# A conv, state-space and attention kernel: two empty steps in the routing, keys fetched one group earlier, and the last two blocks divided in SBUF

## The chip, the cores and the metric

The kernel runs on one core of a Trainium2 chip, in fp32. The metric is the device time of one execution in microseconds. An execution of the kernel before took 5163.62 us (median of three).

## What is computed

The input is an image batch `x` of shape (4, 128, 64, 64). Two residual layers follow each other. Cut to what matters:

```python
# layer 0
x = x + conv_ref(group_norm(x))        # LN, depthwise 3x3 conv, LN, gelu, 1x1 conv, LN,
                                       # a selective scan (16 states) over 4 channel chunks, LN, projection
# layer 1, on tokens (4, 4096, 128)
t = tokens(x)
t = t + attention(ln(t))               # 4 heads of 32, softmax over 4096 keys
t = t + moe(ln(t))                     # 8 experts, the best 2 of a softmax, weights made to sum to 1
x = image(t)
```

Attention divides the weighted sum of values by the sum of the exponentials. The kernel gets both from one matrix product: the values carry columns of ones, so the rows of the accumulator `av` hold, for each of two query blocks, 32 rows of sums and 32 rows that all hold the denominator. The expert part computes, for every token, the sum over the eight experts of (weight x token) times the expert's matrix; weights of unchosen experts are zero.

## The kernel before, in words

**Units.** Each of the 4 batches has 4096 tokens, handled as 8 blocks of 512 (`BLK`). The scan of a block takes 32 slots; a *slot* is one turn of the main loop, and 1024 slots (`END`) hold all scan work. Attention lags behind the scan, because its keys, queries and values come from finished blocks; it goes on for 132 slots after the scan has ended (the *drain*), and a *tail* of expert work follows when attention is done too.

**Order.** Every instruction is issued through one helper (`queued`; all records of the profile carry its line, 406), which chains each engine's instructions in the order of emission. So each engine works strictly in the order in which the slot loop emits. In a slot, that order is: sends that are due; the fetch of scan rows (`rows`, from `bcd`, on SP); the decays (`da`, ACT); on even slots the driven input (`h<-rows,du`, DVE); a second half of a stage on lane X; the scores (`sc`) of the next attention group on PE and their exponentials (`pT`) on ACT; the scan (2.35 us of DVE) on even slots or the product `hc<-rows,h` (1.22 us of DVE) on odd ones; a first half on lane Y; `y<-ident,hc`, by which PE sums an earlier `hc` over its states; a second half on lane Y; the value products (`av`) of the group of the slot before; a first half on lane X.

**Lanes.** All other work is cut into stages at each `yield` of a generator. Two lanes, X and Y, run one task each, two stages for each slot (`advance`): the first, third, ... stage of a task in its first half, the next in its second half. An empty stage lets time pass. Each lane has one PSUM bank for its work (`ps_X`, `ps_Y`). Tasks on lane X are `closed(b, i)`, which ends a block of layer 0 and makes its keys, queries (both as `hi` and `lo` parts) and values (`vst`), and `finished(b, qb, lane)`, called an "out" task: it takes one 512-token block of attention output, divides it (`aT`, `inv`), projects it, adds the residual (`acc`), routes it and applies the experts. An out task may start only in slots 2 to 17 of a block's 32, and only while enough parts of the attention are ready. In the drain and after it both lanes take out tasks. A chain of some 18 small DVE operations in `finished` finds the best two experts and leaves weights in `bothX` or `bothY`; PE transposes those, ACT copies them to `prT`, a DMA stores the weights in DRAM, and DMAs bring them back spread over all partitions (`share`).

**Attention.** The work of a batch is a list of *parts*: a pair of query blocks (`qs`), a head, and one or two blocks of keys (`ks`, `v`). A part of one block has two *groups*, a part of two blocks four; one group is done in each slot (4 passes of PE for `sc`, 8 for `av`). `ready` says whether the blocks that a part needs are closed. The next part's operands are fetched by SP at a set distance from the end of a part; where they were not ready then, the loads are tried again at each group, and at a part's start if need be. Three buffers hold `ks` and `v`, two hold `qs`. Partial sums go to DRAM (`avd`) and come back (`prev`).

**Division.** After the last head of a query pair, the sums of all four heads lie in DRAM (`total`). `inverted` loads the denominators in a compact form (`den`), inverts them, stores them (`inverse`); `finished` loads them spread (`inv`) and multiplies.

The lines that change are shown in these functions:

Of the kernel before, what the change touches and what calls it, by code (L numbers as in the profile page):

```python
# [9 lines left out]
F32 = mybir.dt.float32  # L10
# [7 lines left out]
P = 128  # L18
C = 128
EPS = 1e-5  # L20
BLK = 512
NT = BLK // P
# [3 lines left out]
DH = 32  # L26
NH = 4
NE = 8
# [8 lines left out]
def conv_mamba_attn_moe_kernel(ctx: ExitStack, tc: tile.TileContext, t: dict):  # L37
    nc = tc.nc
    x, out = t["x"], t["out"]
    B, _, L = x.shape  # L40
    NB = L // BLK
# [11 lines left out]
    def load(name, shape=None, src=None, eng=nc.sync, pool=const):  # L53
        src = t[name] if src is None else src
        w = pool.tile(list(shape or src.shape), F32, name=f"w_{name}")
        eng.dma_start(out=w, in_=src)
        return w
# [25 lines left out]
    wv, wp, rw, ew, eb8 = (load(k, eng=late) for k in ("wv", "wp", "rw", "ew", "eb8"))  # L83
# [13 lines left out]
    for j in range(4):  # L97
        r = slice(DI * (j % 2), DI * (j % 2) + DI)
# [301 lines left out]
    class Queue:  # L400
# [7 lines left out]
    tensor, vector, scalar, gpsimd, sync = (  # L408
        Queue(e) for e in (nc.tensor, nc.vector, nc.scalar, nc.gpsimd, nc.sync)
    )  # L410

    def mm(out, lhsT, rhs, start=True, stop=True):
        tensor.matmul(out, lhsT=lhsT, rhs=rhs, start=start, stop=stop)
# [24 lines left out]
    def pool(name, bufs=1, space=None):  # L438
        return main.enter_context(
            tc.tile_pool(name=name, bufs=bufs, **({} if space is None else {"space": space}))  # L440
        )

    att, mix, side = pool("att"), pool("mix"), pool("side")
# [4 lines left out]
    def work(lane, shape=None):  # L448
        return ps_work.tile(shape or [P, BLK], F32, tag=f"work{lane}", name=f"ps_{lane}")

    def tmp(lane, name, shape=None):
        return side.tile(
            shape or [P, BLK], F32, tag=f"tmp{lane}", name=name, bufs=6 if lane == "X" else 4
        )
# [417 lines left out]
    STEP = 2  # L872
# [57 lines left out]
    def attention(b):  # L930

        seen, parts = {}, []
        for q, lo, hi in RUNS:
            known = seen.get(q, 0)
            seen[q] = known + hi - lo
            cuts = [lo, *range(lo + 2 - lo % 2, hi, 2), hi]
            for h in range(NH):  # L940
                for k0, k1 in zip(cuts, cuts[1:]):
                    parts.append((
                        q, h, k0 // 2, k0 % 2, k1 - k0, k0 == lo, k1 == hi, known > 0,
                        seen[q] == NB,
                    ))
        assert all(n == NB for n in seen.values())

        def load(part, qs=None):
            q, h, k, u, n = part[:5]
            if qs is None:  # L950
                qs = queries(b, q, h)
            return qs, keys(b, h, k, u, n), values(b, h, k, u, n)

        prev = None
        ahead = None
        for at, part in enumerate(parts):
            q, h, k, _, n, first, last, more, final = part
            position[0] = b, parts, at
            if ahead is None:
                while not ready(b, part):  # L960
                    yield None
                ahead = load(part)
                for _ in range(2):
                    yield None
            qs, ks, v = ahead
            ahead = None
            for g in range(0, NT * n, STEP):
                if g == 0 and last:
                    prev = None
                    if more:  # L970
                        prev = att.tile([P, BLK], F32, name="prev", bufs=2)
                        sync.dma_start(out=prev, in_=partial.pop((b, q, h)))
                if g >= NT * n - 3 * STEP and ahead is None and at + 1 < len(parts):
                    nxt = parts[at + 1]
                    if ready(b, nxt):
                        ahead = load(nxt, qs if nxt[:2] == (q, h) and not nxt[5] else None)
                scs = []
                for j in range(g, g + STEP):
                    sc = ps_sc.tile([P, 2, BLK], F32, name="sc")
                    for u in range(2):  # L980
                        mm(
                            sc[:, u, :], ks[:, j * P : (j + 1) * P],
                            qs[:, u * BLK : (u + 1) * BLK],
                        )
                    scs.append((v[:, j // NT, j % NT, :], sc))
                yield (
                    b, q, h, scs, first and g == 0, last and g + STEP == NT * n, prev, final,
                )

    sums, partial, total, inverse, later = [None], {}, {}, {}, deque()  # L990
# [9 lines left out]
    def weighted(group):  # L1000
        b, q, h, pTs, first, last, prev, final = group
        if first:
            sums[0] = ps_av.tile([P, BLK], F32, name="av")
        av = sums[0]
        for k, (v, pT) in enumerate(pTs):
            for u in range(2):
                mm(
                    av[64 * u : 64 * u + 2 * DH, :], v, pT[:, u, :],
                    first and k == 0, last and k == STEP - 1,
                )  # L1010
        if last:
            avs = att.tile([P, BLK], F32, name="avs", bufs=2)
            if prev is None:
                scalar.copy(avs, av)
            else:
                vector.tensor_add(avs, av, prev)


            if not final:
                partial[b, q, h] = dram.tile([P, BLK], F32, name=f"avd{q}{h}")  # L1020
                send(partial[b, q, h], avs, 3)
                return
            if h == 0:
                total[b, q] = dram.tile([2, 2, NH, DH, BLK], F32, name=f"total{q}")
            d = total[b, q]
            send(d[:, :, h].rearrange("u k r q -> (u k) r q"), avs, 3)
            if h == NH - 1:
                work_left = inverted(b, q)
                later.extend((slot + n, work_left) for n in (4, 6, 8))

    def inverted(b, q):

# [15 lines left out]
            ))  # L1048
        yield

    def finished(b, qb, lane):

        q, u = divmod(qb, 2)
        td = kqv[b][3]
        s = slice(qb * BLK, (qb + 1) * BLK)
        acc = side.tile([P, NT, C], F32, name="acc", bufs=2)
        aT, inv = tmp(lane, "aT"), tmp(lane, "inv")
        sync.dma_start(out=aT, in_=total[b, q][u, 0].rearrange("h d q -> (h d) q"))
        sync.dma_start(
            out=inv, in_=inverse[b, q][u][:, None, :].to_broadcast([NH, DH, BLK])  # L1060
        )
        sync.dma_start(out=acc.rearrange("p j c -> p (j c)"), in_=td[:, s])
        yield
        yield
        yield
        vector.tensor_mul(aT, aT, inv)
        yield
        ps = work(lane, [P, NT, C])
        for j in range(NT):
            mm(ps[:, j, :], aT[:, j * P : (j + 1) * P], wp)  # L1070
# [4 lines left out]
        ps = transposed(lane, acc)  # L1075
        yield
        xf = tmp(lane, "xf")
        scalar.copy(xf, ps)
        yield
        ps = work(lane, [P, NT, NE])  # L1080
# [41 lines left out]
        vector.tensor_mul(both[:, :, 0:NE], pr, top1.to_broadcast(wide))  # L1122
        vector.tensor_mul(both[:, :, NE:], both[:, :, 0:NE], rs[:, :, None].to_broadcast(wide))
        yield

        ps = work(lane)
        for j in range(NT):
# [2 lines left out]
        prT = tmp(lane, "prT")[0 : 2 * NE, :]  # L1130
# [16 lines left out]


        ps = work(lane)
        mm(ps, eb8, prT[0:NE, :])  # L1150
        yield
        res = tmp(lane, "res")
        vector.tensor_add(res, ps, xf)
        yield
        ahead = deque(share(e) for e in (0, 2))
        yield
        yield
        for e in range(0, NE, 2):
            if e + 4 < NE:
                ahead.append(share(e + 4))  # L1160
            yield
            w = ahead.popleft()
            if e:
                vector.tensor_add(res, res, ps)
            vector.tensor_mul(w, w, xf[:, None, :].to_broadcast([P, 2, BLK]))
            yield
            ps = work(lane)
            for u in range(2):
                mm(ps, ew[:, e + u, :], w[:, u, :], u == 0, u == 1)
        yield  # L1170
        vector.tensor_add(res, res, ps)
        send(out[b][:, s], res, 2)
        yield

# [94 lines left out]
    lanes, done, running = {"X": deque(), "Y": deque()}, set(), {}  # L1269
# [50 lines left out]
    X, Y = lanes["X"], lanes["Y"]  # L1320
# [9 lines left out]
    for k in range(-2, len(blocks)):  # L1330
        if 0 <= k:
            b, i = blocks[k]
            Y.append((("in", b, i, 1), inputs(b, i, 1), [("scan", *blocks[k - 1], 1)] if k else []))
        if k + 2 < len(blocks):
            b, i = blocks[k + 2]
            if k + 2 == 0 or i > 0:
                upper(k + 2)
        if 0 <= k + 1 < len(blocks):
            b, i = blocks[k + 1]
# [19 lines left out]
    END = 2 * len(units)  # L1359

    rows, due, closing, y_of = {}, deque(), deque(), {}
    h_of, slot = {}, 0
# [18 lines left out]
    while (  # L1381
        slot < END or due or closing or summing or waiting or left or later or lanes["X"] or running
    ):
        at, odd = divmod(slot, 2)
# [10 lines left out]
        if unit and not odd:  # L1395
            h = h_of.pop(at)
# [44 lines left out]
    with tc.If(nc.values_load(general[0:1, 0:1]) > 0):  # L1441
# [4 lines left out]
        with tc.For_i(0, B, 1) as b:  # L1446
# [3 lines left out]
                out=t_tok.rearrange("p k c -> p (k c)"),  # L1450
                in_=tsave[bass.ds(b, 1)].rearrange("o p q -> (o p) q"),
            )
            with tc.tile_pool(name="ps_again", bufs=4, space=PSUM) as psum:
                for i in range(NB):
                    ps = anew(t_tok[:, NT * i : NT * (i + 1), :], psum)
# [92 lines left out]
```

## Time and profile before

| | |
|---|---|
| three runs | 5181.4, 5163.62, 5158.14 us; median 5163.62 |
| the profiled execution's own time | 5160.79 us |
| its span | 5158.6 us |
| granted TensorE clock, mean | 0.96 |
| busy: PE, DVE, ACT, POOL | 91%, 74%, 73%, 8% |
| first 645 us | filling: first blocks, attention starts |
| 645 to 4516 us | scan and attention together (the *middle*) |
| 4516 to 5086 us | attention alone (the drain) |
| 5086 to 5158.6 us | the tail |

The page gives the busy share of each engine over the whole span; the windows give it for each stretch. The waits list for one engine what its idle time ended with, in total, in times, and the longest. The chain of waits follows back from the last instruction to what released each step. A timeline row has start, length, engine, operation, and in brackets the idle time before it with what ended it. Consecutive rows of one engine overlap a little[...].

### The profile page before, as it was taken

The page shows a single profiled execution, that of the slowest core. Times are in us where ns is not written, and L with a number is a line of the kernel's source. Part 1 is how long each engine was busy: PE and PEld are TensorE (multiplying, and loading weights), DVE is VectorE, ACT ScalarE, POOL GpSimd, SP SyncE. Part 2 cuts the span into 40 slices and gives each one's busy share as a digit, 9 for nine tenths or more (in the row PEclk, how much of TensorE's full clock was granted, in tenths as well). Part 3 has the DMA queues.
Part 4 walks back from the last instruction along what each step waited for, and adds up shares of the span by engine and source line. Part 5 has one row for each costly group of instructions (what it writes and reads, how often), then busy time and mean ns, then how long its engine had stood idle before and what let it go on. Part 6 is the DMA issues. An engine that isn't in the chain of part 4 may idle for free.

```text
span 5158.6 us, 62573 instructions
## 1 busy us (share of the span) xinstructions
PE 4703.0 (91%) x20684; PEld 2317.3 (45%) x20684; DVE 3835.7 (74%) x5780; ACT 3743.0 (73%) x5700; POOL 433.5 (8%) x483
## 2 busy tenths in 40 slices
PE   4567898999999999999999999999999999999997
PEld 2333444444444444444444444444444444443443
DVE  6988767877778878877788787877888887752422
ACT  4556777887787777787878787787788787765453
POOL 1111111110000110010000100010000001000000
PEclk7778999999999999999999999999999999999997
DMA  4556567677666667676766767667866667764532
GB/s 127 182 189 214 206 212 253 234 235 244 232 226 226 232 230 255 230 241 234 265 236 207 235 218 273 239 227 245 286 219 221 221 234 258 239 212 163 177 130 68
DMA packets 451692, 1131.70 MB, mean 219 GB/s; under 512 B 51857, under 2 KB 135330, under 8 KB 451362
## 3 DMA queue, kind: packets, MB, share of 16 engines
q1 hardware_dynamic: 447296, 1125.96, 64.5%
q8 instruction: 166, 2.72, 0.2%
q10 hardware_dynamic: 4066, 1.67, 0.1%
q14 instruction: 164, 1.34, 0.1%
HBM read 967.22 MB, written 143.39 MB: 215 GB/s over the span
## 4 chain that ended last, share of the span: by engine, by line
PE 58%; DVE 17%; ACT 11%; DMA 7%; issue 4%; POOL 2%; SPq 1%; DVEq 0%; ACTq 0%; POOLq 0%
PE av L406 25%; PE sc L406 14%; PE ps_X L406 9%; PE ps_Y L406 6%; PE y L406 6%; DVE h L406 6%; ACT pT L406 4%; ACT L406 3%; DMA ks<-kd 2%; DVE hc L406 2%; DMA rows<-bcd 1%; ACT xt L406 1%; POOL rsX L406 1%; DMA inv<-inverse 1%; DVE stX L406 1%
## 5 line engine op out<-in xcount | busy, mean ns | idle before, releaser
L406 ACT ACTIVATE pT<-sc 128x1024 f32<-128x1024 f32 x2048 | 1984.9, 1023 | 923.4 <-PE sc L406 922.3
L406 PE MATMUL av<-pT,v 128*64 128x512 f32 x8192 | 2003.1, 610 | 6.4 <-DVE avs L406 6.3
L406 PE MATMUL sc<-qs,ks 128*128 128x512 f32 x4096 | 1298.7, 436 | 91.3 <-DMA ks<-kd 47.8
L406 DVE TENSOR_TENSOR_SCAN h<-da,state,h 128x1025 f32<-128x1025 f32 x512 | 1204.2, 2352 | 91.8 <-ACT h L406 58.2
L406 PEld LDWEIGHTS sc<-qs,ks 128*128 128x128 f32 x4096 | 701.1, 190 | 820.2 <-ACT pT L406 272.7
L406 PEld LDWEIGHTS av<-pT,v 128*64 128x64 f32 x8192 | 500.5, 137 | 838.6 <-issue 813.5
L406 ACT ACTIVATE da<-delta,amat 128x512 f32<-128x512 f32 x1024 | 744.4, 731 | 1.9
L406 PE MATMUL y<-ident,hc 128*128 128x128 f32 x4096 | 622.3, 283 | 58.4 <-DVE hc L406 58.4
L406 DVE TENSOR_TENSOR hc<-rows,h 128x1024 f32<-128x1024 f32 x512 | 624.4, 1220 | 15.7 <-PE y L406 5.4
L406 DVE TENSOR_TENSOR h<-rows,du 128x1024 f32<-128x1024 f32 x512 | 623.4, 1218 | 13.0 <-DMA rows<-bcd 13.0
L406 PEld LDWEIGHTS y<-ident,hc 128*128 128x128 f32 x4096 | 520.8, 147 | 219.0 <-issue 76.0
L406 POOL TENSOR_TENSOR rsX<-rsX,mhalf 128x4 f32<-128x4 f32 x92 | 203.7, 2214 | 2668.0 <-DVE rsX L406 2588.7
L406 ACT ACT_TABLE_LOAD x319 | 409.3, 1283 | 19.5 <-DVE zs L406 14.3
L406 POOL TENSOR_TENSOR rsY<-rsY,mhalf 128x4 f32<-128x4 f32 x100 | 132.1, 1321 | 1812.0 <-DVE shiftY L406 1358.4
L406 DVE TENSOR_TENSOR avs<-av,prev 128x512 f32<-128x512 f32 x96 | 66.1, 689 | 224.4 <-PE av L406 201.4
L406 PE MATMUL ps_X<-share,w_ew 128*128 128x512 f32 x432 | 216.0, 623 | 4.1 <-DVE share L406 3.9
L406 ACT ACTIVATE xt<-ps_Y,shiftY,rsY 128x128 f32<-128x128 f32 x380 | 143.9, 471 | 78.4 <-POOL shiftY L406 70.5
L406 DVE TENSOR_TENSOR share<-share,xf 128x1024 f32<-128x1024 f32 x128 | 155.9, 1218 | 23.5 <-DMA share<-sharesX 13.9
L406 DVE SCALAR_TENSOR_TENSOR cm<-y,w_fc1w,cm 128x512 f32<-128x512 f32 x195 | 145.0, 744 | 8.0 <-ACT y L406 4.5
L406 DVE TENSOR_TENSOR res<-res,ps_X 128x512 f32<-128x512 f32 x108 | 73.7, 683 | 99.9 <-PE ps_X L406 99.7
L406 PE MATMUL ps_Y<-pairs,inxc 128*128 128x512 f32 x256 | 131.2, 638 | 15.8 <-DMA pairs<-xn 10.2
L406 ACT COPY state<-h 128x2 f32<-128x2 f32 x448 | 88.9, 198 | 75.5 <-DVE h L406 75.5
(248 smaller groups left out, 3446.4 us busy)
## 6 DMA issues: line engine op xcount, KB each, us to landing
rows<-bcd SPq DMA_DIRECT2D x1024, 512.0 KB
ks<-kd SPq DMA_DIRECT2D x192, 512.0 KB
qs<-qd SPq DMA_DIRECT2D x161, 512.0 KB
share<-sharesX SPq DMA_DIRECT2D x108, 512.0 KB
v<-vd SPq DMA_DIRECT2D x192, 256.0 KB
ks<-kd SPq DMA_DIRECT2D x128, 256.0 KB
avd<-avs SPq DMA_DIRECT2D x96, 256.0 KB
prev<-avd SPq DMA_DIRECT2D x96, 256.0 KB
```

The lines of the kernel that those rows point to most:

```text
L406: return lambda *args, **kw: queued(op(*args, **kw))
```

## The change

1. **Routing.** Two empty stages stand between the chain on DVE and PE's transposition of its result. With them, an out task is one slot longer.
2. **Keys.** The next part's operands may be fetched from four groups before the end of a part, where it was three.
3. **The last two blocks.** The last query pair of the last batch no longer goes through DRAM. `divided` takes each head's sums as they leave the accumulator, inverts the whole tile (denominators stand 32 times, so every row has its own) and multiplies each block's 32 rows into a tile of the out task. `finished` takes that tile, and does not wait for stages that load and multiply.
4. **Experts after the scan.** From slot `END` on, the terms of the expert sum are accumulated in one PSUM bank, and one addition at the end replaces the five that stood between the products.

```diff
-                if g >= NT * n - 3 * STEP and ahead is None and at + 1 < len(parts):
+                if g >= NT * n - 4 * STEP and ahead is None and at + 1 < len(parts):
...
+            if b == B - 1 and q == NB // 2 - 1:
+                divided(b, q, h, avs)
+                return
             d = total[b, q]
...
+    def divided(b, q, h, avs):
+
+        if h == 0:
+            quotient.extend(mix.tile([P, BLK], F32, name="xin", bufs=2) for _ in range(2))
+        rec = att.tile([P, BLK], F32, name="prev", bufs=2)
+        vector.reciprocal(rec, avs)
+        for u in range(2):
+            r, d = 64 * u, 64 * u + DH
+            vector.tensor_mul(
+                quotient[u][DH * h : DH * h + DH, :], avs[r : r + DH, :], rec[d : d + DH, :]
+            )
+        if h == NH - 1:
+            for u in range(2):
+                lanes["X"].append((
+                    ("out", b, 2 * q + u),
+                    lambda lane, i=2 * q + u, a=quotient[u]: finished(b, i, lane, a), [],
+                ))
...
-    def finished(b, qb, lane):
+    def finished(b, qb, lane, aT=None):
...
+        if aT is None:
+            aT, inv = tmp(lane, "aT"), tmp(lane, "inv")
...
+            yield
+            yield
+            yield
+            vector.tensor_mul(aT, aT, inv)
+            yield
         ps = work(lane, [P, NT, C])
...
         vector.tensor_mul(both[:, :, NE:], both[:, :, 0:NE], rs[:, :, None].to_broadcast(wide))
         yield
+        yield
+        yield
 
         ps = work(lane)
...
-        mm(ps, eb8, prT[0:NE, :])
-        yield
-        res = tmp(lane, "res")
-        vector.tensor_add(res, ps, xf)
+        mm(ps, eb8, prT[0:NE, :], True, slot < END)
+        yield
+        one = slot >= END
+        if not one:
+            res = tmp(lane, "res")
+            vector.tensor_add(res, ps, xf)
...
-            if e:
+            if e and not one:
                 vector.tensor_add(res, res, ps)
...
-            ps = work(lane)
+            if not one:
+                ps = work(lane)
             for u in range(2):
-                mm(ps, ew[:, e + u, :], w[:, u, :], u == 0, u == 1)
+                mm(
+                    ps, ew[:, e + u, :], w[:, u, :], u == 0 and not one,
+                    u == 1 and (not one or e + u == NE - 1),
+                )
         yield
-        vector.tensor_add(res, res, ps)
+        if one:
+            res = tmp(lane, "res")
+            vector.tensor_add(res, ps, xf)
+        else:
+            vector.tensor_add(res, res, ps)
```

More of the change, by code (lines that the diff above doesn't have):

```diff
@@ L1029, in weighted @@
                 later.extend((slot + n, work_left) for n in (4, 6, 8))
+    quotient = []
+    def divided(b, q, h, avs):
[14 more added lines that the diff above has]
+                ))
     def inverted(b, q):
@@ L1056, in finished @@
         acc = side.tile([P, NT, C], F32, name="acc", bufs=2)
[L1057 to L1061, printed above, removed]
-        sync.dma_start(out=acc.rearrange("p j c -> p (j c)"), in_=td[:, s])
-        yield
[L1064 to L1067, printed above, removed]
+        sync.dma_start(out=acc.rearrange("p j c -> p (j c)"), in_=td[:, s])
+        if aT is None:
+            aT, inv = tmp(lane, "aT"), tmp(lane, "inv")
+            sync.dma_start(out=aT, in_=total[b, q][u, 0].rearrange("h d q -> (h d) q"))
+            sync.dma_start(
+                out=inv, in_=inverse[b, q][u][:, None, :].to_broadcast([NH, DH, BLK])
+            )
[4 more added lines that the diff above has]
+            yield
         ps = work(lane, [P, NT, C])
@@ L1166, in finished @@
             yield
-            ps = work(lane)
+            if not one:
+                ps = work(lane)
             for u in range(2):
-                mm(ps, ew[:, e + u, :], w[:, u, :], u == 0, u == 1)
+                mm(
+                    ps, ew[:, e + u, :], w[:, u, :], u == 0 and not one,
+                    u == 1 and (not one or e + u == NE - 1),
+                )
         yield
-        vector.tensor_add(res, res, ps)
+        if one:
[3 more added lines that the diff above has]
+            vector.tensor_add(res, res, ps)
         send(out[b][:, s], res, 2)
```

## The prediction

> **What bounds the kernel now.** I read the page first (which engine), then the windows (which stage), the waits of TensorE in each window, the chain of the tail, and last the timelines around single waits.
>
> ```profile
> PE 4703.0 (91%) x20684; PEld 2317.3 (45%) x20684; DVE 3835.7 (74%) x5780; ACT 3743.0 (73%) x5700; POOL 433.5 (8%) x483
> ...
> 645.00:4516.00 3871.00, 3692.01 (x16667) 1822.82 (x16668) 3110.39 (x4545) 3057.51 (x4674) 341.81 (x365) 0.99 0.70 237
> 4516.00:5086.00 570.00, 561.03 (x2298) 242.51 (x2298) 193.34 (x446) 316.55 (x362) 15.43 (x14) 0.99 0.46 157
> 5086.00:5158.60 72.60, 35.66 (x92) 17.54 (x88) 29.27 (x83) 3.37 (x7) 2.02 (x2) 0.63 0.29 92
> ```
>
> Columns of the window rows: length, busy time of PE, PEld, DVE, ACT and POOL, granted clock, DMA share, GB/s. The middle (scan and attention together) keeps PE busy 95% of the time at clock 0.99, the drain (attention alone) 98%. There only PE's own waits can be won. The tail of 72.6 us has PE half idle: latency rules it.
>
> ```profile
> PE sc L406 <- DMA ks<-kd: 33.0, 14, 4.6
> PE ps_X L406 <- DVE bothX L406: 19.4, 17, 2.0
> ...
> PE y L406 <- DVE hc L406: 5.8, 3, 1.9
> ...
> PE ps_X L406 <- ACT prT L406: 0.9, 3, 0.3
> ```
>
> These are PE's waits in the middle (total us, times, longest). The second and fourth are what the empty steps address, the first what the earlier key fetch addresses; the third is the one I expect to grow. In the drain bothX has 2.1 and bothY 0.4.
>
> ```profile
> 5087.53 0.59 ACT avs L406
> 5088.14 5.87 DMA total<-avs
> 5094.06 0.55 SPq L406
> 5094.66 2.00 DMA den<-total
> 5096.69 0.36 DVE den L406
> 5097.07 1.42 DMA inverse<-den
> ...
> 5100.06 8.75 DMA inv<-inverse
> 5108.91 0.70 DVE aT L406
> 5109.65 2.08 PE ps_X L406 x8
> ```
>
> This is the chain of the tail (start, length): from the last av to the output projection, 21 us pass of which some 18 are DMA round trips.
>
> **1. Division in SBUF (gain).** Removed: all between 5088.12 (ACT has copied avs) and 5109.65 (second projection begins). In its place: one reciprocal of 128x512 and two multiplies. The reciprocal has two near rows: 128x4 takes 0.178 us, 128x32 takes
>
> ```profile
> L406 DVE RECIPROCAL den<-den x16: 341/345/353, 1283.3 to 5096.7; 128x32 f32<-128x32 f32 x16
> ```
>
> so (345-178)/28 = 5.96 ns for each element of a partition, and 178 + 508 x 5.96 = 3.2 us. The Trainium skill ("VectorE: DVE Perf Modes", "First, the fixed hardware budget") says that the divide repeats 8 times; at the page's 0.96 GHz 512 x 8 give an estimate of 4.3 us. Were it an ordinary 128x512 operation, 0.69 (aT's row). I take 3.2, since it is read off this chip: 5088.12 + 3.2 = 5091.35, multiplies (0.69 each) to 5092.05 and 5092.7; the first projection (2.08, at half clock) runs to 5094.1, and the second starts there: 5109.65 - 5094.1 = **15.5 us**. With 4.3 it would be 14.4, with 0.69 about 18. Behind it nothing changes in length: the share loads, both routing chains (18 operations of 0.19 on DVE) and 48.95 us to the end stay. The two empty steps cost nothing there, since both lanes' chains stand one behind the other on DVE and not in the slots. The other three heads' reciprocals (3.2 + 1.4 each) lie in the drain, where DVE has 193 of 570 us and PE's next operand from DVE is over a slot away; uncovered, up to 2 us. The expert sums kept in PSUM in the drain drop DVE additions; PE runs without a gap from 5137.88 to the last sum, so 0 (bounds 0 and -1.5).
>
> **2. Two empty steps (gain, smaller than the wait).** PE's transposition now stands one slot later in its order, so the 19.4 us go. But the chain also stands ahead of hc on DVE, and PE's next slot needs hc:
>
> ```profile
> 2737.13 1.22 DVE L406 TENSOR_TENSOR hc<-rows,h 128x1024 f32<-128x1024 f32 x1
> ...
> 2737.27 0.60 PE L406 MATMUL ps_X<-ident,bothX 128*16 128x128 f32 x4 [1.80 <-DVE bothX L406]
> ...
> 2739.07 0.60 PE L406 MATMUL y<-ident,hc 128*128 128x128 f32 x4
> ```
>
> PE waited 1.80 to 2737.27. Without that wait it does sc (1.01 of own time) and the xt transposition (0.43) from 2735.47 and stands at y at 2736.91, while hc ends at 2738.34: a wait of 1.43. So 1.80 becomes 1.43, one of 0.8 becomes 0.4, one of 0.4 nearly nothing (nine of the 17 are of 1.8 to 2.0). Over all 17, 14.3 of 19.4 stay, as hc waits: gain **5.1**. In the drain there is no hc: **2.4**. prT: **0.9**. Everything behind the steps (prT's copy, its DMA, the share loads) comes a slot later in SP's and ACT's order with the same spacing; PE waits for share only 2.7 in the middle, so 0.
>
> The clock. One bothX wait, 2.0 us to 1417.4, stands ahead of a dip:
>
> ```profile
> 1414.50:1417.90 3.40, 1.40 (x11) 0.46 (x8) 2.99 (x15) 2.31 (x7) 0.81 (x5) 1.00 0.30 108
> 1417.90:1421.30 3.40, 3.40 (x14) 2.58 (x12) 3.30 (x3) 2.96 (x4) 0.00 (x0) 0.51 0.40 146
> ```
>
> 3.4 us at half clock cost **1.7**. The Trainium skill ("TensorE: Matmul & The Clock Gate", "What's actually happening") ties the drop to an idle window of about 3.4 us: by it a wait of 2.0 costs no clock (gain 0 here), and it speaks against the change in item 4, where new waits are longer. The trace decides: 1.7 here, waits of 1.8 did not dip, key waits from 3.3 up were followed by 3.4 to 6.8 us at half clock.
>
> **3. Keys four groups ahead.** In the order of the changed program 187 of 313 key loads go out one slot earlier, all behind parts of two k-blocks (4 groups). A part of one block has two groups, so its load stands at its first group with 3 or 4 alike. Each of the 14 key waits of 33.0 us follows a part of one block or is a first load. The loads that move have some 15 us of lead against 6.7 to 10.5 us to land. So **0**; bounds +3 (SP's queue and DMA are fuller at 0.70) and -3.
>
> **4. Two key loads that go out later (loss).** An output task is now one slot longer. Where it starts early in a block, the `closed` task behind it on lane X starts at slot 18 of 32 instead of 17 (13 to 15 times), and with it `ready`. (What `closed` issues moves along: the load of xr and the sends of tt, tr, hi, lo and vst on SP, three operations on POOL, which is 8% busy: 0 beyond what follows.) Twice the next part waits for just that: slot 699 becomes 700, 923 becomes 924. The first, before:
>
> ```profile
> 3107.52 0.88 SPq L406 DMA_DIRECT2D ks<-kd  x1
> ...
> 3113.22 1.65 SPq L406 DMA_DIRECT2D rows<-bcd  x2
> ...
> 3116.61 1.20 PE L406 MATMUL sc<-qs,ks 128*128 128x512 f32 x4
> ```
>
> Lead 9.09 us, no wait (the second: 4137.04 to 4145.21, 8.17). A slot later the keys are queued behind the rows issue, which waits for hc: about 3115.3 and 4144.6, landing 6 to 8 us later: PE waits some 4.3 to 6.3 and 7, with y, av and the next pT behind it, plus 1.7 to 3.4 each at half clock: **-16.5** (from -8 to -28).
>
> **5. hc late in slot 27 (loss).** In those blocks hi/lo of `closed` (two operations) stand ahead of hc in slot 27 where vst (0.69) stood. The slack of y behind hc there was 1.0, hc comes 1.4 later: 0.4 x 11 = 4.4. In five blocks whose output task starts at slot 12 (slots 411, 443, 539, 667, 795) res (0.68 at 1939.69) gets a share multiply (1.22) beside it; the slack was 0.11 (hc ends 1941.51, y starts 1941.62): 1.1 x 5 = 5.5. Together **-9.9** (from 0 to -20).
>
> **Sum.** Gain 15.5 + 5.1 + 2.4 + 0.9 + 1.7 = 25.6; loss 16.5 + 9.9 = 26.4; net 0.8 slower. On the profiled execution (5160.79; its span 5158.6 and 2.2 around it): 5161.6. That run lies 2.8 below the median of 5163.62, so the median to expect is **5164**.
>
> **The rivals.** A measurement of this kernel tells about 0.5% (25.8 us) from no change.
> - *As summed* (0.50): 5152 to 5177, no change.
> - *Slower: the shifted `closed` tasks cost more* (0.32). Place: slots 27 and the key loads of slots 700 and 924. Price: 14 us a load (8 of wait, SP's queue, 3.4 at half clock) and 1.5 for each of 16 hc, together 52 against 25.6: 5164 + 26 = 5190. It turns the sign when items 4 and 5 pass 25.6, and 0.5% at about 51. For: DMA is 0.70 busy, no slack at slot 27, and a slip of `ready` can reach other loads. Against: key loads after parts of two blocks become earlier.
> - *Faster: the waits are simply gone* (0.16). PE's other work in the slot covers hc, and DMA lands the two late loads in the 5 us they have: 15.5 + 19.4 + 2.4 + 0.9 + 1.7 = 40 at most; with item 5 and a part of item 4 left, some 30: 5134. For: keys have landed in 6 us before. Against: the hc row at 2737.13 above, and `rows` ahead of the keys on SP.
> - *The division is off the path* (0.02): the final heads' projections wait for something else, the tail gains 0: 5180.
>
> Chances: slower by over 0.5% is 0.23 (most of the second), faster 0.14 (most of the third), same 0.63. Range 5136 to 5196; what is as summed alone, 5152 to 5177.
>
> **What would show it.** After: tail from last av to the end near 55.5 us instead of 71, with a reciprocal of 128x512 near 3.2; bothX gone from PE's waits, y <- hc up from 5.8 to about 30; key waits up from 14 to 16 of them and by about 11 us, at slots 700 and 924 (near 3115 and 4143 us); granted clock in the middle 0.99 still. Wrong if y <- hc stays near 6 (then faster by 14), or the middle lengthens by over 30 us.

## The result, and the profile after

The changed kernel takes 5174.68 us (median of 22 runs) against 5162.62 of the kernel before (22 runs): a ratio of 1.0023, with a 95% interval of 1.0017 to 1.0030. It is 12 us slower, within the 0.5% that the prediction called no change, and 11 above its 5164. The profiled execution took 5177.44 (span 5175.6). One of the 22 executions of the kernel called "change, acc last" below took 17853 us, and that one is left out of its ratio.

The windows show where. The same attention groups that stood between 645 and 4516 us now end at 4552, and the last av, 5087.5 before, ends at 5126.1. Columns as before: length, busy PE, PEld, DVE, ACT, POOL, granted clock, DMA share, GB/s.

```profile
645.00:4552.00 3907.00, 3710.79 (x16663) 1830.41 (x16664) 3109.84 (x4543) 3058.00 (x4674) 349.95 (x365) 0.98 0.70 235
4552.00:5126.10 574.10, 566.76 (x2308) 244.43 (x2307) 188.20 (x424) 316.69 (x364) 15.61 (x14) 0.99 0.46 155
5126.10:5175.60 49.50, 28.84 (x86) 14.86 (x84) 26.99 (x75) 3.37 (x7) 2.02 (x2) 0.73 0.29 98
```

The middle has grown by 36 us for the same work. Half of it is waiting: PE's idle time is 3907.0 - 3710.8 = 196.2, against 3871.0 - 3692.0 = 179.0 before. The other half is PE being busy longer, 3710.8 against 3692.0, with as many matmuls: the granted clock is 0.98, where it was 0.99. How much of that is clock can be estimated from windows of 1 us, each weighted by its clock: PE's busy time in them times (1 - clock) sums to 39.6 us before and 53.4 after, so to about 14 of these 18.8. The drain is about 3 longer. The tail, 71.1 before, is 49.5.

PE's waits in the middle (total us, times, longest):

```profile
PE sc L406 <- DMA ks<-kd: 41.4, 16, 5.9
...
PE y L406 <- DVE hc L406: 20.7, 27, 2.0
...
PE ps_X L406 <- DVE aT L406: 13.8, 8, 3.3
```

bothX is gone from this list, as announced. hc rose from 5.8 to 20.7, the keys from 33.0 to 41.4. One line was not foreseen: aT is 13.8, where it was

```profile
PE ps_X L406 <- DVE aT L406: 5.3, 4, 2.2
```

The two late key loads are there. First the timeline of SP, then rows of PE's, in the changed kernel:

```profile
3128.28 0.38 SPq L406 DMA_DIRECT2D vd<-vst  x1
3129.41 0.54 SPq L406 DMA_DIRECT2D rows<-bcd  x1
3130.04 0.56 SPq L406 DMA_DIRECT2D ks<-kd  x1
```

```profile
3136.58 2.04 PE L406 MATMUL sc<-qs,ks 128*128 128x512 f32 x4 [4.62 <-DMA ks<-kd]
...
4182.61 2.05 PE L406 MATMUL sc<-qs,ks 128*128 128x512 f32 x4 [5.86 <-DMA ks<-kd]
```

The keys go out behind vst's send and a rows load, land 6.5 us later, and PE has waited 4.62 us. The sc that follows takes 2.04 where it took 1.20: PE has come back at half clock. Each of the two stretches at half clock lasts almost 7 us and begins some 2.5 us after PE has begun to wait:

```profile
3134.60:3141.50 6.90, 4.92 (x14) 2.80 (x16) 4.41 (x3) 2.64 (x4) 0.00 (x0) 0.51 0.95 353
...
4179.10:4186.10 7.00, 3.49 (x10) 2.34 (x12) 4.03 (x3) 2.02 (x3) 0.00 (x0) 0.51 1.01 383
```

And the wait that took the place of bothX, in the block shown before (timeline of all engines):

```profile
2750.78 0.19 DVE L406 TENSOR_TENSOR bothX<-bothX,rsX 128x32 f32<-128x32 f32 x1
2750.89 1.22 DVE L406 TENSOR_TENSOR hc<-rows,h 128x1024 f32<-128x1024 f32 x1
...
2752.16 0.66 PE L406 MATMUL y<-ident,hc 128*128 128x128 f32 x4 [1.16 <-DVE hc L406]
```

PE no longer waits 1.80 for bothX; it waits 1.16 for the hc that stands behind the chain on DVE.

The tail's timeline goes as drawn: the reciprocal, and the projections from the two tiles that the multiplies fill.

```profile
5126.79 3.35 DVE L406 RECIPROCAL prev<-avs 128x512 f32<-128x512 f32 x1 [41.84 <-ACT avs L406]
5130.18 1.40 DVE L406 TENSOR_TENSOR xin<-avs,prev 32x512 f32<-32x512 f32 x2
5130.91 1.36 PE L406 MATMUL ps_X<-w_wp,xin 128*128 128x128 f32 x7 [4.79 <-DVE xin L406]
```

For aT's later wait there is a candidate on SP (timeline of all engines). In the changed `finished` the loads of aT and inv have moved into a branch below acc's load, so they stand behind it:

```profile
2325.20 0.54 SPq L406 DMA_DIRECT2D rows<-bcd  x1
2325.79 0.60 SPq L406 DMA_DIRECT2D acc<-td  x1
2327.06 0.33 SPq L406 DMA_DIRECT2D aT<-total  x1
2327.75 0.57 SPq L406 DMA_DIRECT2D inv<-inverse  x1
...
2338.59 0.69 DVE L406 TENSOR_TENSOR aT<-aT,inv 128x512 f32<-128x512 f32 x1 [3.43 <-DMA inv<-inverse]
...
2339.33 0.98 PE L406 MATMUL ps_X<-w_wp,aT 128*128 128x128 f32 x3 [3.32 <-DVE aT L406]
```

DVE waits for inv's landing, and PE for DVE. Before, the order was aT, inv, acc, and the same wait of PE was 2.22 (rows of SP, then PE):

```profile
2311.64 0.62 SPq L406 DMA_DIRECT2D aT<-total  x1
2313.02 0.57 SPq L406 DMA_DIRECT2D inv<-inverse  x1
2313.76 0.72 SPq L406 DMA_DIRECT2D acc<-td  x1
...
2324.69 1.16 PE L406 MATMUL ps_X<-w_wp,aT 128*128 128x128 f32 x8 [2.22 <-DVE aT L406]
```

The move is in the diff, though its lines are left out of the cut shown above; the prediction did not cost it. These rows show the order, not yet that it is the cause.

### The profile page after: what moved, and what is told of

Read it like the earlier page. It is cut to its first block, busy times and chain, and to the rows that moved or that the text cites. A ratio compares the mean times of both kernels' runs of the same rounds, so it can differ in the third digit from the quotient of the medians.

```text
span 5175.6 us, 62520 instructions
## 1 busy us (share of the span) xinstructions
PE 4720.9 (91%) x20684; PEld 2324.3 (45%) x20684; DVE 3827.9 (74%) x5749; ACT 3743.5 (72%) x5700; POOL 441.8 (9%) x483
## 5 line engine op out<-in xcount | busy, mean ns | idle before, releaser
L406 ACT ACT_TABLE_LOAD x319 | 409.3, 1283 | 19.5 <-DVE zs L406 14.3
L406 DVE TENSOR_TENSOR share<-share,xf 128x1024 f32<-128x1024 f32 x128 | 155.3, 1221 | 75.7 <-DMA share<-sharesY 40.7
L406 PE MATMUL ps_Y<-pairs,inxc 128*128 128x512 f32 x256 | 131.1, 637 | 14.3 <-DMA pairs<-xn 8.7
L406 PEld LDWEIGHTS ps_X<-share,w_ew 128*128 128x128 f32 x432 | 74.1, 191 | 151.0 <-issue 91.4
```

Of the source, the lines that this page charges most:

```text
L406: return lambda *args, **kw: queued(op(*args, **kw))
```

## The experiments

Twelve kernels ran, each timed against the kernel before on the same chip. The theory to test (A): the change wins in the tail, and loses it because closed tasks start a slot late, because acc's load is ahead of aT's, and because each new long wait also costs half-clock time. All results together; the kernel before had medians of 5163.1 beside the first four experiments of the table, 5167.1 beside the next four and 5163.0 beside the last four, so the ratios are the numbers to compare, and gains below are worked from them:

| kernel | median, us | ratio to before | 95% interval |
|---|---|---|---|
| the whole change | 5174.7 | 1.0023 | 1.0017 to 1.0030 |
| change, acc last | 5169.6 | 1.0012 | 1.0006 to 1.0019 |
| before, acc first | 5171.1 | 1.0015 | 1.0007 to 1.0023 |
| empty steps alone | 5191.9 | 1.0055 | 1.0041 to 1.0069 |
| division and PSUM sums | 5152.0 | 0.9979 | 0.9970 to 0.9988 |
| empty steps, outputs from slot 1 | 5161.3 | 0.9991 | 0.9981 to 1.0000 |
| keys alone | 5157.9 | 0.9985 | 0.9976 to 0.9994 |
| change, acc last, no empty steps | 5146.8 | 0.9957 | 0.9944 to 0.9970 |
| change, acc last, outputs from slot 1 | 5143.9 | 0.9956 | 0.9943 to 0.9968 |
| two key loads late | 5174.8 | 1.0019 | 1.0011 to 1.0027 |
| outputs from slot 1 alone | 5157.0 | 0.9987 | 0.9974 to 1.0000 |
| division alone | 5152.2 | 0.9981 | 0.9971 to 0.9992 |
| acc last, no empty steps, outputs from slot 1 | 5134.6 | 0.9940 | 0.9926 to 0.9953 |

**acc last, in the changed kernel.** In `finished`:

```diff
-        sync.dma_start(out=acc.rearrange("p j c -> p (j c)"), in_=td[:, s])
         if aT is None:
...
                 out=inv, in_=inverse[b, q][u][:, None, :].to_broadcast([NH, DH, BLK])
             )
+            sync.dma_start(out=acc.rearrange("p j c -> p (j c)"), in_=td[:, s])
...
+        else:
+            sync.dma_start(out=acc.rearrange("p j c -> p (j c)"), in_=td[:, s])
```

> The changed kernel with one thing put back: the load of acc goes out behind those of aT and inv, as before. Theory A (the change also moved acc's load ahead of aT and inv on SP, so aT comes about 1.4 us later, PE waits for it and the clock dips): aT's waits in the middle fall from 13.8 to about 5 us, half-clock time falls too, and the whole is some 20 us below the changed kernel, about 5154 (8 below the kernel before). Theory B (aT is late because keys are fetched earlier and the DMAs are fuller): no change from the changed kernel, about 5174. Theory C (the wait is real, the clock's loss is chance): about 10 below it, 5164.

aT's wait in the middle falls to

```profile
PE ps_X L406 <- DVE aT L406: 7.2, 4, 3.4
```

and the kernel is about 5 us faster than the changed one: far from A's 20, between B and C. Nor do aT and inv go out 1.4 us later: over the blocks of the middle, inv is issued on average 0.8 us after the first of these three loads in the kernel before and in this one, and 1.4 in the changed kernel.

**acc first, in the kernel before.**

```diff
+        sync.dma_start(out=acc.rearrange("p j c -> p (j c)"), in_=td[:, s])
         aT, inv = tmp(lane, "aT"), tmp(lane, "inv")
...
-        sync.dma_start(out=acc.rearrange("p j c -> p (j c)"), in_=td[:, s])
```

> The kernel before with acc's load put ahead of those of aT and inv, and nothing else. Theory A: 20 us slower than before, about 5183, aT's waits in the middle from 5.3 to about 14 us and more windows at half clock. Theory B: as before, 5163. Theory C: 10 slower, 5173.

aT's wait rises to

```profile
PE ps_X L406 <- DVE aT L406: 12.7, 9, 2.7
```

from 5.3 with keys still three ahead, so B is out: the order on SP makes aT late, not the keys. inv is issued 1.5 us after the first of the three loads here, 0.8 before. The price is 8 us (0.15%, interval 4 to 12), not 20. The expectation had put all half-clock time that follows an aT wait in the changed kernel on acc's account; the 8 is about the wait itself (7.4). Theory C was nearer.

**The empty steps alone.**

```diff
         vector.tensor_mul(both[:, :, NE:], both[:, :, 0:NE], rs[:, :, None].to_broadcast(wide))
         yield
+        yield
+        yield
```

> The kernel before with the two empty steps alone. Theory A (the two key loads of slots 700 and 924 go out late: 15.5 us; bothX 19.4 turns into hc waits of 10.2; hc and share in slots 27 and 28 cost 8; drain gains 2.5): about 12 us slower than before, 5175, with key waits near 41 us and no bothX. Rival D (the steps take the bothX waits away and what is slower in the changed kernel comes from its other parts): 10 to 20 us faster, 5143 to 5153.

This is the change's loss, and more than twice what A said: 28 us (interval 21 to 36). Rival D is out, they are not a gain. PE's waits in its middle and drain:

```profile
PE sc L406 <- DMA ks<-kd: 47.4, 17, 6.2
...
PE y L406 <- DVE hc L406: 20.8, 27, 1.9
...
PE ps_Y L406 <- DVE gmv L406: 11.0, 3, 4.2
...
PE ps_X L406 <- DVE share L406: 5.8, 8, 0.9
```

Against the kernel before over the same stretch, keys have +14, hc +15, gmv (the group norm of the next batch) +4.7, share +3; bothX has -21.5. That is a net 15. Beside it PE is busy longer, as the window with the same 16667 matmuls as before shows, 3710.7 us where it was 3692.0; how much of that is clock is in the table at the end of this section.

```profile
646.50:4557.50 3911.00, 3710.70 (x16667) 1827.40 (x16668) 3112.03 (x4545) 3057.67 (x4676) 347.27 (x365) 0.98 0.70 235
```

**Empty steps, with closed tasks back on time.** Output tasks may start a slot earlier, so with the extra slot they end when they did before:

```diff
-                    and not (2 <= slot % (2 * NST) < NST + 2 and stocked(LEAD))
+                    and not (1 <= slot % (2 * NST) < NST + 2 and stocked(LEAD))
```

> The kernel before with the two empty steps, and output tasks allowed to start from slot 1 of a block (it was 2), so that the closed tasks behind them start at slot 17 as before and the keys of slots 699 and 923 go out on time. Theory A (most of the steps' 29 us come from closed tasks a slot late: 15.5 for the two loads, 3.4 for hc in slot 27, with their half-clock time): about 8 slower than before, 5171, with no new key wait at those two places. Rival D (the later routing itself costs it, wherever closed starts): 25 to 29 slower, 5188 to 5192.

It is 5 us faster than before (0.9991, interval up to 1.0000), 33 below the empty steps alone, where A had expected 8 slower than before. So the loss of the steps is that what follows them on lane X, in the output task and in the closed task behind it, comes late. Key waits are back at 33.5 and hc at 5.8. But the chain's 3.6 us on DVE show up elsewhere: PE's waits for xt rise from 12.4 to

```profile
PE ps_Y L406 <- ACT xt L406: 29.9, 19, 6.2
```

In this block the chain ends at 2742.35, and DVE goes on with:

```profile
2742.27 2.35 DVE L406 TENSOR_TENSOR_SCAN h<-da,state,h 128x1025 f32<-128x1025 f32 x1
2744.53 0.86 DVE L406 BATCH_NORM_STATS2 stY<-ps_Y 128x6 f32<-128x128 f32 x4
...
2745.96 1.98 POOL L406 TENSOR_TENSOR rsY<-rsY,mhalf 128x4 f32<-128x4 f32 x1 [18.81 <-DVE shiftY L406]
...
2748.31 1.50 ACT L406 ACTIVATE xt<-ps_Y,shiftY,rsY 128x128 f32<-128x128 f32 x4 [2.13 <-POOL shiftY L406]
...
2749.86 0.66 PE L406 MATMUL ps_Y<-ident,xt 128*128 128x128 f32 x4 [1.42 <-ACT xt L406]
```

Lane Y's statistics stand behind the chain and the scan, POOL's power ends late, ACT waits for POOL, and PE for ACT.

**Outputs from slot 1, alone.** The same one-line edit on the kernel before.

> The kernel before with output tasks allowed from slot 1 of a block, and nothing else; closed tasks then start at slot 16. Theory A (what helped with the empty steps was closed tasks back on time, not the earlier output tasks): within 5 us of before. Rival G (earlier output tasks help by themselves): 10 or more faster.

It is about 6.7 us faster (interval from 0 to 13), between the two expectations. It does not undo that lateness on lane X was the steps' loss, but a part of the 33 us, perhaps 7, may be this edit's own. And it takes bothX's waits away without any empty step, for the start of an output task sets which slot the chain falls into. PE's waits in its middle:

```profile
PE ps_Y L406 <- ACT xt L406: 25.6, 27, 6.2
...
PE ps_X L406 <- DVE lo L406: 3.1, 4, 1.7
...
PE ps_X L406 <- DVE bothX L406: 1.5, 4, 0.4
```

Before, bothX had 19.4, and the others

```profile
PE ps_Y L406 <- ACT xt L406: 12.4, 7, 6.2
PE ps_X L406 <- DVE lo L406: 11.6, 16, 1.7
```

**Two key loads late, alone.**

```diff
-                    if ready(b, nxt):
+                    if slot not in (699, 923) and ready(b, nxt):
```

> The kernel before, in which the key loads of slots 699 and 923 are held back to slots 700 and 924, and nothing else. Theory A (prediction's item 4, measured as 15.5 in the changed kernel's trace): 12 to 18 slower than before, with two new key waits of 4 to 7 us and two windows of half clock behind each. Rival F (these two are only a third of what late closed tasks cost, and the half clock behind them is chance): 5 to 10 slower.

It is 10 us slower (0.19%, interval 6 to 14), nearer to F. The two waits are

```profile
3126.71 1.17 PE L406 MATMUL sc<-qs,ks 128*128 128x512 f32 x4 [1.89 <-DMA ks<-kd]
...
4160.09 2.05 PE L406 MATMUL sc<-qs,ks 128*128 128x512 f32 x4 [4.01 <-DMA ks<-kd]
```

After the first sc takes 1.17, at full clock; after the second 2.05. In the changed kernel the same loads cost waits of 4.62 and 5.86, with half clock at each that by the estimate above takes another 2.5 and 1.7: some 15 us. The first of them was issued there 1.9 us before PE began to wait and took 6.5 to the start of sc; here it was 2.9 us and 4.8. So the loads are a third to a half of the empty steps' loss.

**Division and PSUM sums; division alone.** The division's and the expert sums' parts of the diff on the kernel before, with acc's load last; in the second, with `one` always false.

> The kernel before with the division in SBUF for the last two blocks and the expert sums of the drain kept in PSUM, acc's load last as before, no empty steps, keys three ahead. From the changed kernel's trace (49.5 us from the last av to the end, where it was 71.1): 21.6 us faster than before, about 5141. The prediction's sum: 15.5 faster, 5147. Rival: the division's DVE work in the drain costs PE what the tail wins, below 8 faster.

> The kernel before with the division in SBUF alone; the expert sums of the drain are added on DVE as before. Theory A (the division is the gain, the sums in PSUM are worth 0 to 2): 9 to 12 faster, and the tail from the last av to the end 50 to 52 us. Rival H (the sums in PSUM shorten the last eight products from 1.9 to 1.7 us each, and more): tail 54 us or longer, 5 to 7 faster.

Both are 10 to 11 us faster (intervals 6 to 15 and 4 to 15), half of the 21.6 and short of the 15.5, as the theory for the division alone said; and the sums in PSUM are worth nothing that can be measured. The tail from the last av to the end is 49.9 and 52.4 us. That the whole gains only half of it has two reasons that the traces show. The profile of the kernel before had an unusually long tail, 71.1: the six other kernels here with the old division have 66.6 to 69.0, 68.0 on average, and the seven with the new one 49.4 to 52.4, 50.8 on average, so the tail's gain is about 17, not 21.6. And a part is lost in the drain, where the first head's reciprocal stands ahead of the aT of a block's output task:

```profile
4930.72 3.35 DVE L406 RECIPROCAL prev<-avs 128x512 f32<-128x512 f32 x1 [5.14 <-ACT avs L406]
4934.11 1.38 DVE L406 TENSOR_TENSOR xin<-avs,prev 32x512 f32<-32x512 f32 x2
4935.52 0.69 DVE L406 TENSOR_TENSOR aT<-aT,inv 128x512 f32<-128x512 f32 x1
...
4936.27 1.08 PE L406 MATMUL ps_X<-w_wp,aT 128*128 128x128 f32 x5 [2.33 <-DVE aT L406]
```

PE waits 2.33, and the eight passes then take 1.72 where they take 1.05 at full clock, the first of 3.4 us at half clock: some 4 us in all. 17 less 4 is 13, inside the interval. The changed kernel does not pay this: in its drain the wait is 0.2.

**Keys alone.**

```diff
-                if g >= NT * n - 3 * STEP and ahead is None and at + 1 < len(parts):
+                if g >= NT * n - 4 * STEP and ahead is None and at + 1 < len(parts):
```

> The kernel before with keys four groups ahead, and nothing else. Theory A (the loads that move were not late, the late ones do not move): 5160 to 5166, key waits in the middle 33 us as before. Rival E (what is missing in the sum of the parts is the keys' gain: steps +28.8, division -11, acc +5 to +8 against +11.6 for all): 11 to 14 faster, about 5150.

It is 8 us faster (interval 3 to 12), between A and E. The waits do not say where: PE's key waits are 33.9, as before, and its profiled execution (5161.3) is as long as that of before. What the earlier loads win is left open.

**The change without the empty steps; with them, repaired.** The first has acc last and no empty steps. The second keeps the steps, with acc last and outputs from slot 1.

> The changed kernel without the two empty steps and with acc's load last: division in SBUF, expert sums in PSUM, keys four ahead. Theory A: as the division alone, 11 faster than before, 5152. Rival E: 22 to 25 faster, about 5139.

> The whole changed kernel with its two side effects taken back: acc's load last, and output tasks allowed from slot 1, so that closed tasks start on time. Theory A: 5 to 8 (acc) and 19 (closed) below the changed kernel, about 5149, 14 faster than before. Rival D: only acc's part, about 5168. If the empty steps lose more than they win even then, it stays above the kernel without them.

They take 5146.8 and 5143.9, ratios 0.9957 and 0.9956: two ways to the same time. The first, 22 faster than before, is what rival E said: the division's 11 and the keys' 8 add up. It also measures the steps a second time: against the changed kernel with acc last (1.0012) it is 28 us faster, as much as the steps cost alone. The second is faster than A said (14): with both side effects taken back, the whole change is 23 us faster than before instead of 12 slower, and as fast without its empty steps.

**Without empty steps, and outputs from slot 1.** In the expectation, gate_alone is the kernel of "outputs from slot 1, alone".

> The kernel with division in SBUF, expert sums in PSUM, keys four ahead, acc's load last and output tasks from slot 1, without the empty steps. If gate_alone is a gain, this is the fastest, below the 5144 of the kernel with the steps; if theory A holds it stands with the kernels with and without the steps, 5140 to 5150.

It has the lowest time of all: 5134.6, 0.9940 of before, 28 to 31 us faster. It stands some 8 below the one with empty steps, but the two intervals overlap (0.9926 to 0.9953, and 0.9943 to 0.9968), so that the steps still cost something there is not shown.

**The middle in all traces.** Each profile can be cut from the same point (645 us in the kernel before, shifted with its first sc) to where PE has done 16667 matmuls. All in us; the last column is the estimate from windows of 1 us:

| kernel | length | PE idle | PE busy | lost to half clock |
|---|---|---|---|---|
| before | 3870.7 | 179.0 | 3691.7 | 39.6 |
| the whole change | 3908.7 | 196.5 | 3712.3 | 53.5 |
| change, acc last | 3900.7 | 192.0 | 3708.6 | 51.3 |
| empty steps alone | 3910.6 | 200.4 | 3710.2 | 51.1 |
| empty steps, outputs from slot 1 | 3875.3 | 180.6 | 3694.7 | 40.6 |
| before, acc first | 3880.5 | 188.0 | 3692.5 | 39.2 |
| two key loads late | 3882.1 | 189.0 | 3693.1 | 40.7 |
| the seven others | 3861 to 3874 | 170 to 179 | 3690 to 3697 | 39 to 45 |

Only the three kernels in which lane X runs late after the empty steps have PE busy 17 to 21 us longer than before, and only they lose over 50 us to half clock: three profiles of three, and none of the other eleven. Starting the output tasks a slot earlier takes both away. So the clock's loss belongs to the steps and is hardly chance. It comes neither from acc (39.2) nor from the two key loads alone (40.7); these two edits add waits. In the changed kernel it lies in 26 stretches of half clock where there were 21, each with a wait of PE of 1.5 us or more beside it. What makes up the other 5 to 7 us of busy time is not known.

## Why the prediction was right, and where it was not

The forecast of no change held, and its ground too: a gain in the tail, eaten by what the empty steps make late. But the middle grew by 36 us, more than the 30 that the prediction had named as a sign of being wrong, its clock fell to 0.98 where 0.99 was to stay, and hc's waits rose to 20.7, not to about 30. Not all terms had their size, and that the errors nearly cancelled was luck.

- *Division.* Right on the path, too large in the whole. The reciprocal took 3.35 (forecast 3.2 by the rows; the estimate from the Trainium skill's "VectorE: DVE Perf Modes", "First, the fixed hardware budget", was 4.3). The second projection starts 6.2 after the last av instead of 22.2, 16.0 earlier against 15.5. Behind it 43.3 us pass to the end, where 48.95 were to stay; that length was unusual, for the six other kernels with the old division have 44.3 to 46.9. The "uncovered, up to 2 us" for the other heads did happen in the kernels with the division and no empty steps, with half-clock time behind it: some 4. The whole is worth 10 to 11, not 15.5.
- *Empty steps.* The mechanism was right: bothX gone, hc in its place. What hc took back was 11.3 us in the slots of the chain, not 14.3; prT's wait rose from 0.9 to 1.9 instead of going. With items 4 and 5 the prediction has 16.3 of loss for the steps (26.4 less 5.1, 2.4, 0.9 and 1.7); alone they cost 28.
- *Keys ahead.* Wrong in size: 0, bounds -3 to +3, and alone it wins 3 to 12. Its reason held as far as it goes (the 33 us of key waits stay).
- *Two late loads.* Right: some 15 in the changed kernel against 16.5, waits of 4.62 and 5.86 and half clock at both. Alone they cost 10.
- *hc in slot 27.* Right in place and nearly in size: twelve waits of 0.27 to 0.40 there (forecast 0.4 x 11). In the five blocks with a share multiply PE waits 0.9 for the share itself, not for hc: 4.5 against 5.5.
- *What was not in the sum.* First, acc's load ahead of aT and inv: the diff puts those two DMAs behind it on SP, and the prediction costed only what the diff removes. It cost 5 to 8 us. Second, the clock. Items 2 and 4 counted the half clock of the waits that they named, a net 2 to 5 us of loss; the estimate for the middle is 14, of which the two loads are 4. By the longest wait beside each stretch, another 3 belong to other key waits and 3 to gmv. The remaining 4 are a net of all other waits, of which those for gn, xt and pT gain most although they are in sum about as long as before; why they have half clock beside them more often stays open. Third, the waits for the next batch's group norm (gmv), 2 us longer in the changed kernel and 4.7 with the steps alone; no run tells why.

The parts measured alone (steps, keys, division, acc) add up to 28 - 8 - 11 + 8 = 17 against 12 for the whole, within their intervals. Against the forecast's 0.8 that is 12 more loss for the steps, 8 for acc and 4 to 5 less gain for the division, with 8 more gain for the keys: the errors were each larger than the sum they were to give.

The rival that ended slower had the right direction: what the steps make late on lane X does cost more than the sum had. Its size was too large. It took 52 us of loss against the steps' own gains of 10, so 42 for the steps, and 28 were measured, between its figure and the sum's 16.

## What to carry to other kernels

A wait that a delayed consumer avoids is worth only what does not stand behind the same producer: look up what its engine does next, and who needs that. An empty step in a task that shares a lane delays the tasks behind it too: here the two steps took 19.4 us of waits away, gave 11.3 back in the same slots, and cost 28 us in all. Shifting the start of the task took the same waits away without a step, and won 0 to 13 us. And when a diff moves a DMA's issue past others on one queue, cost it against every load that it passes: here one line cost 8 us.

## What the runs showed of the hardware that was not expected

- A reciprocal on DVE has cost 178 ns for 4 elements in each partition, 345 for 32 and 3353 for 512: 6.3 ns for each element beyond the first 32, while a multiply of 128x512 takes 690. One time per element, drawn from the two small tiles, was 4% low.
- Waits near 2 us sometimes have half clock beside them and sometimes do not: 1.89 for keys in one run did not, nor did bothX's 1.80, while hc's 1.95 at 3165.6 us of the kernel before has it, and so has a key wait of 1.81 at 1663.3 us, so the prediction's "waits of 1.8 did not dip" holds for bothX alone. In the middle of the kernel before, the changed one and that with two loads late, every wait of 2.6 us or more has half clock beside it.
- The stretch up to the first sc at 345.7 us is the same instructions in the kernel before and in that with the division, yet it ended 6.8 us later in the latter's profile. In the fourteen profiles it ends between 345.3 and 353.0. Single profiles of this kernel differ by that much before any edit acts, so differences below 10 us in the whole time are read from the medians of several runs, not from one trace beside another.
